# One fused graph network on one core: the opening and the convolution with degrees put in another order

## The chip, the cores and the metric

The kernel runs on one core of a Trainium2 chip. Its time is the device time in microseconds of one launch; lower is better. Several runs of the same program give a median. Besides the runs there is one profiled execution, whose trace lists every instruction of the engines: TensorE (PE, and PEld for its weight loads), VectorE (DVE), ScalarE (ACT), GpSimd (POOL) and SyncE (SP, which here only issues transfers). Each engine takes its own instructions strictly in order, as the kernel's lists stand, and waits for the others by semaphores.

## The reference, cut to what matters

512 nodes with 512 features, 16,896 edges sorted by destination. Four blocks follow each other, each with a residual:

```python
h = relu(layernorm(x)); x = x + attention_block(h, adjacency)      # L0: a graph transformer
h = relu(layernorm(x)); x = x + gin_block(h, edges)                # L1: sums over neighbours, two layers
h = relu(layernorm(x)); x = x + gcn(h, edges)                      # L2: convolution with degrees
h = relu(layernorm(x)); x = x + rgcn(h, edges, edge_types)         # L3: relations with 30 bases

def gcn(X, W, b, edge_index):        # loops are appended to the edges
    deg = segment_sum(1, dst);  dinv = rsqrt(deg)
    out = segment_sum((X @ W)[src] * dinv[src] * dinv[dst], dst) + b
    return where(out >= 0, out, 0.01 * out)
```

The relational block needs a weight matrix for each relation, which is a sum over 30 basis matrices of 512 x 512 (60 MB for its two layers).

## The kernel before, in words

**Edges become count matrices.** The kernel turns the edge list into dense 512 x 512 count matrices, one for each edge type, and every block then multiplies by them. For each chunk of 128 edges it makes two one-hot blocks, `hd` (destinations, 32 or 64 columns, on VectorE) and `hs` (sources, 512 columns, on ScalarE for four chunks in seven, on VectorE for three). A count matmul (`count`, line 556) multiplies them into a PSUM bank. There are 132 chunks and 204 count matmuls. The rows are made up to `BEHIND` = 7 chunks ahead of the counts.

**Stray edges.** Since the edges are sorted, each chunk is matched against only some groups of 32 destinations. `lim` holds the lowest and highest destination that a chunk may have, and `look_for_strays` (lines 406 to 420) sets `flag` if any edge lies outside. Line 460 reads the flag on all engines, and a branch leads to a slow path, which these inputs don't take. What follows in program order can't start on an engine before that engine has read the flag.

**The opening.** Around that check stand: the casts of the index (line 390) and their transposes into `key`; moments of the four tiles of x (lines 342 and 343); `first_norm` (a root, two small VectorE instructions and the normed tile `h`, lines 378 to 381); `flip`, which transposes a tile with four matmuls (line 331) and evicts it with ScalarE (line 335). GpSimd fills `lim`, adds the tile's offset to three parts of it (line 144), counts out `it` (line 150) and fills `apart` with ones (line 459). VectorE casts `it` into `iot` (line 415), the row that all one-hot blocks are compared with.

**Counts beside projections.** The loop over counts also carries the rest of the attention block's beginning. `plan` says after which count which piece comes: "p" half a tile of the projections q, k and v (lines 478 and 491, four passes of fp32 each), "G" a basis step, "s" and "S" scores. The first piece stands after count number `FIRST`, the others are spread evenly from there to the end of the counts. In the first eleven counts the planner of the framework may order instructions by its own costs; after that, and wherever an instruction is wrapped in `on(...)`, program order holds.

**Basis tiles.** SyncE streams the basis matrices in a fixed order through four buffers of 1 MB; the next load starts when a buffer is free. `basis_step` multiplies a tile into the PSUM bank `bas` (line 242). After the last step of a bank, ScalarE evicts it (line 247) and issues a DMA of 256 KB from its own queue (line 248). Other basis tiles are summed by VectorE (line 266).

**Convolution with degrees** (lines 1017 to 1060). It follows the second layer of L1, whose `settle` adds the last slices to x (line 855). The last basis step of that layer and the gate rows (line 803) come first. Then for every tile t of x: moments, a root (lines 1034 and 1045), `by = dinv / root` and `nm = -mean * by` (lines 1036 to 1038), the normed tile twice on ScalarE (line 1043: once rounded to fp32r as the high part, once in full), and the difference as the low part on VectorE (line 1046). `gather` (line 941) multiplies high and low parts of two tiles with the counts into the four `acc` banks. ScalarE and VectorE then copy the banks (lines 1053 and 1055) for the product with W.

## Time and profile before

| | |
|---|---|
| Median of three runs | 510.85 us (510.64 to 511.44) |
| Profiled execution, its own time | 512.15 us |
| Its span in the trace | 510.2 us |
| TensorE busy | 482.8 us (95%) |
| VectorE busy | 399.8 us (78%) |
| ScalarE busy | 196.1 us (38%) |
| GpSimd busy | 37.8 us (7%) |
| Moved by DMA | 94.06 MB, mean 184 GB/s |

The span runs from the first instruction of the trace to the last; the rest of the profiled execution's time lies around it. In the profile a name such as `hs<-iot,key` is output and inputs of an instruction; L547 is line 547 of the kernel before. The row of 40 slices gives the busy share of an engine in tenths, each slice 12.76 us long. A timeline has start, length, engine, line, operation and count, and in brackets how long the engine was idle before it and what ended that. A list of waits has the waiting instruction, the one waited for, the sum of the time, how often, and the longest.

### The profile page before, as it was taken

The page shows a single profiled execution, that of the slowest core. Times are in us where ns is not written, and L with a number is a line of the kernel's source. Part 1 is how long each engine was busy: PE and PEld are TensorE (multiplying, and loading weights), DVE is VectorE, ACT ScalarE, POOL GpSimd, SP SyncE. Part 2 cuts the span into 40 slices and gives each one's busy share as a digit, 9 for nine tenths or more (in the row PEclk, how much of TensorE's full clock was granted, in tenths as well). Part 3 has the DMA queues.
Part 4 walks back from the last instruction along what each step waited for, and adds up shares of the span by engine and source line. Part 5 has one row for each costly group of instructions (what it writes and reads, how often), then busy time and mean ns, then how long its engine had stood idle before and what let it go on. Part 6 is the DMA issues. An engine that isn't in the chain of part 4 may idle for free.

```text
span 510.2 us, 5732 instructions
## 1 busy us (share of the span) xinstructions
PE 482.8 (95%) x2014; PEld 247.4 (48%) x2014; DVE 399.8 (78%) x748; ACT 196.1 (38%) x318; POOL 37.8 (7%) x81
## 2 busy tenths in 40 slices
PE   2999999999999999999999999998699999999996
PEld 2333333255564547864445445543454584446642
DVE  6847487879999879999885964897459999998611
ACT  4876779724444213223422134124633610123000
POOL 7000000100000021300130000000010100000000
PEclk9999999999999999999999999999999999999999
DMA  7999768998978499686552696877933966520011
GB/s 244 273 249 258 176 175 195 218 261 192 226 162 193 109 214 297 226 216 228 189 176 83 153 233 213 293 198 188 255 103 124 308 177 222 180 82 3 0 42 41
DMA packets 42951, 94.06 MB, mean 184 GB/s; under 512 B 2113, under 2 KB 2567, under 8 KB 42919
## 3 DMA queue, kind: packets, MB, share of 16 engines
q1 hardware_dynamic: 34682, 68.17, 50.5%
q0 software_dynamic: 5712, 21.07, 14.2%
q10 hardware_dynamic: 2525, 4.39, 2.6%
q8 instruction: 20, 0.33, 0.3%
q14 instruction: 12, 0.10, 0.1%
HBM read 88.38 MB, written 5.24 MB: 183 GB/s over the span
## 4 chain that ended last, share of the span: by engine, by line
PE 65%; DVE 18%; ACT 9%; DMA 3%; issue 2%; ACTq 0%; DVEq 0%; SPq 0%
PE pr L318 19%; PE acc L1125 11%; PE pg L318 9%; PE acc L1091 5%; PE ps L478 4%; DMA basis<-in_basis 3%; PE bas L242 3%; DVE sc L642 3%; ACT sc L643 3%; ACT hs L547 3%; DVE sc L660 3%; PE ao L556 2%; PE acc L941 2%; DVE half L636 2%; DVE wrel L266 2%
## 5 line engine op out<-in xcount | busy, mean ns | idle before, releaser
L266 DVE SCALAR_TENSOR_TENSOR wrel<-basis,scal,wrel 128x1024 f32<-128x1024 f32 x60 | 74.1, 1282 | 2.5 <-DMA basis<-in_basis 2.5
L547 ACT ACTIVATE hs<-iot,key 128x512 f16<-128x512 f16 x75 | 48.8, 712 | 5.7 <-PE ao L556 4.9
L543 DVE TENSOR_SCALAR hd<-iot,key 128x32 f16<-128x32 f16 (+1 forms) x132 | 33.4, 295 | 15.6 <-PE ao L556 15.4
L242 PE MATMUL bas<-basis,wide 120*32 120x512 f32 (+1 forms) x320 | 43.5, 600 | 1.6 <-DMA basis<-in_basis 0.9
L266 DVE SCALAR_TENSOR_TENSOR w<-basis,scal,w 128x1024 f32<-128x1024 f32 x32 | 39.3, 1277 | 0.0
L556 PE MATMUL ao<-hs,hd 128*32 128x512 f16 x204 | 25.9, 396 | 2.8 <-ACT hs L547 2.6
L643 ACT ACTIVATE sc<-sc 128x2048 f32<-128x2048 f32 (+1 forms) x10 | 15.7, 1568 | 32.7 <-DVE sc L642 32.6
L478 PE MATMUL ps<-bigB,w 128*128 128x512 f32 x56 | 27.2, 614 | 0.9 <-ACT bigD L481 0.6
L318 PE MATMUL pr<-bigE,w 128*128 128x512 f32 x48 | 21.6, 596 | 0.0
L1175 DVE TENSOR_TENSOR u<-acc,x 128x512 f32<-128x512 f32 (+1 forms) x5 | 2.8, 584 | 23.5 <-PE acc L1125 23.5
L318 PE MATMUL pr<-bigD,w 128*128 128x256 f32 x88 | 20.2, 380 | 0.0
L549 DVE TENSOR_SCALAR hs<-iot,key 128x512 f16<-128x512 f16 x57 | 19.3, 347 | 0.0
L642 DVE TENSOR_TENSOR sc<-sc,half 128x2048 f32<-128x2048 f32 (+1 forms) x10 | 18.6, 1864 | 0.2
L660 DVE TENSOR_TENSOR sc<-sc,rec 128x2048 f32<-128x2048 f32 x8 | 18.3, 2286 | 0.0
L627 PE MATMUL psc<-bigC,bigD 64*128 64x256 f32 x128 | 18.1, 402 | 0.0
L318 PEld LDWEIGHTS pr<-bigD,w 128*128 128x128 f32 x88 | 16.6, 190 | 3.0 <-ACT bigE L885 0.8
L556 PEld LDWEIGHTS <-hd 128*32 128x32 f16 x204 | 6.1, 94 | 24.4 <-issue 15.7
L350 ACT ACTIVATE sd<-mv,eps 128x1 f32<-128x1 f32 x16 | 4.7, 296 | 34.4 <-DVE mv L343 33.4
L318 PE MATMUL pr<-w,bigE 128*128 128x512 f32 x40 | 17.8, 592 | 0.0
L658 DVE RECIPROCAL rec<-ps 128x256 f32<-128x256 f32 x8 | 14.0, 1752 | 3.7 <-PE ps L654 3.7
L478 PEld LDWEIGHTS ps<-bigB,w 128*128 128x128 f32 x56 | 9.6, 189 | 14.9 <-issue 11.1
L629 ACT COPY sc<-psc 128x1024 f32<-128x1024 f32 x16 | 15.6, 1007 | 2.6 <-issue 1.6
(317 smaller groups left out, 958.1 us busy)
## 6 DMA issues: line engine op xcount, KB each, us to landing
basis<-in_basis SPq DMA_DIRECT2D x32, 960.0 KB
basis<-in_basis SPq DMA_DIRECT2D x23, 1024.0 KB
basis<-in_basis SPq DMA_DIRECT2D x16, 448.0 KB
summed<-sums ACTq DMA_DIRECT2D x16, 256.0 KB
w<-in_W POOLq DMA_DIRECT2D x4, 1024.0 KB, 7.1
row<-in_rows POOLq DMA_DIRECT2D x12, 256.0 KB, 8.0
wrel<-summed POOLq DMA_DIRECT2D x4, 512.0 KB, 7.9
w<-in_conv_W1T POOLq DMA_DIRECT2D x2, 1024.0 KB, 5.9
```

The source lines that it names most:

```text
L242: tc.keep_in_program_order(nc.tensor.matmul(sums[0][32 * j:32 * j + 32, :], lhsT=lhsT, rhs=t[:k, j, :], start=(g == 0), stop=(g == STEPS + ...
L266: on(nc.vector.scalar_tensor_tensor(to[r][:, i:i + 2, :], t[:, i:i + 2, :], scal[:, at:at + 1], to[r][:, i:i + 2, :], op0=ALU.mult, op1=AL ...
L318: nc.tensor.matmul(p, lhsT=lhsT, rhs=rhs, start=(i == 0), stop=(i == len(pairs) - 1))
L478: on(nc.tensor.matmul(p, lhsT=w[:, k, ts(m)], rhs=made["hT"][:, k, :], start=(k == 0), stop=(k == T - 1)))
L543: keep(nc.vector.tensor_scalar(hd[:, :w], iot[:, GW * groups_of[c][0]:GW * groups_of[c][0] + w], key[:, 0, c:c + 1], key[:, 2, c:c + 1], o ...
L547: keep(nc.scalar.activation(hs, iot, AF.Sign, bias=key[:, 3, c:c + 1]))
L556: keep(nc.tensor.matmul(cnt[b][GW * (g % T):GW * (g % T) + GW, :], lhsT=hd[:, at:at + GW], rhs=hs, start=(c == in_bank[g][b][0]), stop=(c ...
L642: on(nc.vector.tensor_sub(s, s, half[:, 0:1, :].to_broadcast([P, H // pieces, NH])))
L643: on(nc.scalar.activation(s, s, AF.Exp, scale=HD ** -0.5))
L660: on(nc.vector.tensor_mul(self.sc, self.sc, rec[:, None, :].to_broadcast([P, H, NH])))
L1091: nc.tensor.matmul(self.out[t], lhsT=self.hT[:, k, ts(t)], rhs=self.root[:, k, :], start=(k == 0), stop=False)
L1125: nc.tensor.matmul(self.out[t], lhsT=self.uT[r][:, k, ts(t)], rhs=wrel[r][:, k, :], start=False, stop=(r == 1 and k == T - 1))
```

## The change

In the opening:

- GpSimd's arithmetic goes. The additions to `lim` move to VectorE ahead of everything else there; `apart` is filled by a ScalarE activation (the root of 0 times eps plus 1); the third cast of the index and `iot` go to ScalarE too.
- All four tiles of x are normed and transposed ahead of the check for strays, in written order. The roots are taken out of `first_norm` into `root`.
- The check compares with a fused operation for each end (`tensor_tensor_reduce`, largest excess in `some`), and two one-column matmuls add both. The upper limit becomes inclusive for it. The slow path makes its own list of strays.
- All counts are in program order, the first eleven too, and so is `select`, which prepares the weights of the basis steps. `FIRST` becomes 4.
- The first bias rows are asked for later in the program.

In the convolution with degrees:

- The last basis step stands behind the gate rows, and its eviction and DMA (`leave`) behind the whole norm.
- Moments and roots run ahead over all four tiles, high parts follow two tiles behind; then full parts and differences of tiles 0 and 1, a gather, both parts of tiles 2 and 3, a gather.

The diff, cut to its core (`on(...)` around instructions of `select`, and the slow path, are left out):

```diff
-        nc.gpsimd.tensor_scalar_add(over_tiles[:, :, t, :], over_tiles[:, :, t, :], float(P * t))
+        on(nc.vector.tensor_scalar_add(over_tiles[:, :, t, :], over_tiles[:, :, t, :], float(P * t)))
...
-    rows = Stream([row_load(i) for i in range(len(ROWS))], 4)
+    rows = Stream([row_load(i) for i in range(len(ROWS))], 0)
+    rows.ahead = 4
...
+                def leave(n=n, bank=sums[0]):
+                    o = spool.tile([P, 512], F32, tag="sums", name="sums")
+                    keep(nc.scalar.copy(o, bank))
+                    nc.scalar.dma_start(summed[l][n], o)
+
+                if held is None:
+                    leave()
+                else:
+                    held.append(leave)
...
+    def root(t):
+        on(nc.scalar.activation(by4[:, t, 0:1], mv4[:, t, 1:2], AF.Sqrt, bias=eps))
...
+    on(nc.scalar.activation(apart.rearrange("p t n -> p (t n)"), eps.to_broadcast([P, T * N]), AF.Sqrt,
+                            bias=ones, scale=0.0))
     for i in range(3):
-        on(nc.vector.tensor_copy(kn[:, i, :], idx[:, i, :]))
+        on((nc.scalar.copy if i == 2 else nc.vector.tensor_copy)(kn[:, i, :], idx[:, i, :]))
...
+    on(nc.scalar.copy(iot, it))
     moments(mv4[:, 0, :], x[:, 0, :], on)
+    root(0)
     on(nc.vector.tensor_copy(key[:, 0:2, :], pk[:, 0:2, :]))
     on(nc.vector.tensor_scalar(key[:, 2, :], pk[:, 2, :], 0.0, LESS, op0=ALU.is_equal, op1=ALU.max))
     moments(mv4[:, 1, :], x[:, 1, :], on)
-    for t in range(2):
-        first_norm(t)
+    first_norm(0)
+    root(1)
     moments(mv4[:, 2, :], x[:, 2, :], on)
+    root(2)
+    first_norm(1)
+    flip(h, 0, hT0, on)
+    moments(mv4[:, 3, :], x[:, 3, :], on)
+    root(3)
+    first_norm(2)
+    first_norm(3)
+    flip(h, 1, hT0, on)
+    on(nc.vector.tensor_scalar(key[:, 3, :], key[:, 1, :], -1.0, 0.5, op0=ALU.mult, op1=ALU.add))
...
+    some = rp.tile([P, 2], F32, name="some")
+    for i, ends in enumerate(((lim[:, 0, :], key[:, 0, :]), (key[:, 0, :], lim[:, 1, :]))):
+        on(nc.vector.tensor_tensor_reduce(stray, *ends, 1.0, 0.0, op0=ALU.subtract, op1=ALU.max,
+                                          accum_out=some[:, i:i + 1]))
+    for t in (2, 3):
+        flip(h, t, hT0, on)
+    p = ps()
+    for i in range(2):
+        on(nc.tensor.matmul(p[0:1, 0:1], lhsT=some[:, i:i + 1], rhs=ones, start=(i == 0), stop=(i == 1)))
+    on(nc.vector.tensor_copy(flag, p[0:1, 0:1]))
...
-    nc.gpsimd.memset(apart, 1.0)
...
     bases.start(AHEAD)
+    rows.start(4)
...
-    made["h"], made["hT"] = h, big("B")
-    for t in range(T):
-        flip(made["h"], t, made["hT"])
+    made["h"], made["hT"] = h, hT0
...
-    FIRST = 9
+    FIRST = 4
...
-        keep = on if n > 10 else loose
...
         if l:
-            basis_step(1)
+            held = []
             gates = gate_rows(1, [apart.bitcast(F32).rearrange("p t n -> p (t n)")[:, N * r:N * r + N] for r in range(2)])
             next(gates)
+            basis_step(1, on, held)
...
     for t in range(T):
+        moments(mv[:, t, :], x[:, t, :], on)
+        root(t)
+        if t:
+            scale(t - 1)
+        if t > 1:
+            normed_to(xn[0], t - 2)
+    scale(3)
+    for t in (0, 1):
+        normed_to(h, t)
         on(nc.vector.tensor_sub(xn[1][:, t, :], h[:, t, :], f32(xn[0][:, t, :])))
-        if t % 2:
-            gather((t - 1, t), apart=True)
+    gather((0, 1), apart=True)
+    for to in (xn[0], h):
+        for t in (2, 3):
+            normed_to(to, t)
+    for t in (2, 3):
+        on(nc.vector.tensor_sub(xn[1][:, t, :], h[:, t, :], f32(xn[0][:, t, :])))
+    gather((2, 3), apart=True)
+    for leave in held:
+        leave()
```

In the new convolution `root(t)` is the square root of a tile's variance, `scale(t)` the three small VectorE instructions for `by` and `nm`, and `normed_to(to, t)` one activation that writes the normed tile into the high part or in full into `h`.

## The prediction

> **What bounds the kernel now.** I read the page's busy rows and slices first, then the windows by stage, then the timeline at the two places that the change touches, then who waited there.

> ```profile
> span 510.2 us, 5732 instructions
> PE 482.8 (95%) x2014; PEld 247.4 (48%) x2014; DVE 399.8 (78%) x748; ACT 196.1 (38%) x318; POOL 37.8 (7%) x81
> PE   2999999999999999999999999998699999999996
> ```

> TensorE is busy 482.8 of 510.2 us, so 27.4 us are idle. The row of slices shows two dips: the first slice (0 to 12.8 us) and the slices near 360 us. These are the two places that the change rewrites. Everywhere else the order of instructions is kept, apart from where projections fall between counts, and TensorE stays the bound, so a shift made at either place should travel to the end.

> ```profile
> core 0: us, PE busy (x) PEld busy (x) DVE busy (x) ACT busy (x) POOL busy (x), PEclk, DMA share, GB/s
> 12.00:24.00 12.00, 11.06 (x38) 4.23 (x39) 10.33 (x58) 9.08 (x16) 1.01 (x5) 1.00 1.02 284
> 24.00:44.00 20.00, 19.46 (x90) 6.65 (x90) 11.93 (x46) 14.73 (x25) 0.77 (x1) 1.00 1.00 248
> ...
> 356.00:372.30 16.30, 11.34 (x58) 8.09 (x59) 8.37 (x26) 9.34 (x17) 0.00 (x0) 1.00 1.00 258
> ```

> From 24 us on TensorE idles 0.5 us in 20, while VectorE has 8 us to spare. In the convolution with degrees (356 to 372.3) TensorE idles 5 of 16.3 us. The waits of that stretch say on whom:

> ```profile
> PE acc L941 <- ACT bigC L1043: 4.6, 3, 1.9
> ```

> The timeline of the convolution (start, length, engine, line):

> ```profile
> 355.42 0.69 DVE L855 TENSOR_TENSOR x<-x,pg 128x512 f32<-128x512 f32 x1 [1.60 <-PE pg L331]
> 356.31 1.07 PE L242 MATMUL bas<-basis,wide 112*32 112x512 f32 x8 [0.93 <-DMA basis<-in_basis]
> 357.43 0.59 ACT L247 COPY sums<-bas 128x512 f32<-128x512 f32 x1 [2.76 <-PE bas L242]
> 358.42 0.48 ACT L1034 ACTIVATE sd<-mv,eps 128x1 f32<-128x1 f32 x2 [0.40 <-ACT sums L247]
> 359.39 0.81 ACT L1043 ACTIVATE bigC<-x,nm,by 128x512 fp32r<-128x512 f32 x1 [0.49 <-DVE nm L1038]
> 368.38 0.81 ACT L1043 ACTIVATE bigC<-x,nm,by 128x512 fp32r<-128x512 f32 x1 [1.27 <-DVE nm L1038]
> 370.32 1.98 PE L941 MATMUL acc<-R,F 128*128 128x512 f32 x8
> ```

> The last slice of x is whole at 356.11. The first square root waits for the eviction of the basis bank (line 247) to 358.42, and then each of the four tiles passes root, scale, high part, full part and difference nearly one after another, at about 3 us a tile. TensorE ends at 372.30.

> The opening, same columns:

> ```profile
> 10.51 0.14 DVE L418 CAST flag<-ps 1x1 int32<-1x1 f32 x1
> 12.07 1.09 PE L331 MATMUL ps<-ident,bigA 128*128 128x128 f32 x4 [1.86 <-DVEq L461]
> 13.09 0.62 PE L556 MATMUL ao<-hs,hd 128*32 128x512 f16 x3
> 14.45 0.59 PE L556 MATMUL ao<-hs,hd 128*32 128x512 f16 x1 [0.75 <-ACT hs L547]
> 17.35 3.68 PE L478 MATMUL psc<-bigB,w 128*128 128x512 f32 x4
> 21.29 1.98 PE L478 MATMUL psc<-bigB,w 128*128 128x512 f32 x4
> ```

> The flag is out at 10.65 and every engine reads it: TensorE resumes 1.42 later. Counts start at 13.09, with gaps and two transposed tiles among them.

> **The change, part 1: the convolution.** I walk the new order with the durations of the rows above, from x whole at 356.11. VectorE: moments of a tile take 0.9 (statistics 0.69, aggregation 0.18), a scale 0.6 (three small instructions, 358.75 to 359.35). Order: moments 0, 1, scale 0, moments 2, scale 1, moments 3, scales 2 and 3. Moments end at 357.05, 357.85, 359.3 and 360.65; scale 0 at 358.47, scale 1 at 359.85. ScalarE now has nothing of the basis bank ahead of it, but its order is root 0, 1, 2, then high part 0: root 2 waits for moments 2, so high part 0, ready at 358.5, goes at 359.6 (1.1 us given away) and ends at 360.4. Root 3 waits until 360.67, high part 1 ends at 361.8. From there six activations back to back, 0.72 apart as at 365.58 and 366.30: full parts 0 and 1 by 363.1, high parts 2 and 3 by 364.6, full parts 2 and 3 by 366.0. Differences (0.69): 363.15, 363.85, 366.0, 366.7.
> TensorE, four matmuls at 0.23 to 0.25 a piece (12 took 2.96): high 0 360.4 to 361.4; high 1 361.8 to 362.75; low 0 363.15 to 364.1; low 1 to 365.05; high 2 and 3 to 366.95; low 2 and 3 to 368.85. Against 372.30 that is **-3.4 us**. Bounds: the 28 matmuls after high 1 make 6.6 us, so no better than 368.4 (-3.9); with 0.3 us lost at each of three handovers, -2.5.
> The basis step itself moves behind the gate rows on TensorE, still ahead of the gathering matmuls. It waits for a load that landed at 356.2 and lasts 1.07; the first gathering matmul wants TensorE at 360.4, so the load may be 3.1 us later before it costs. Its eviction and its DMA (0.59 and 0.33 on ScalarE's queue) now stand behind full part 3, at 366.0 to 366.95, and ahead of two gate copies (1.05) to 368.0; the copy of the first sum wants ScalarE at 368.15. The cover is thus 0.15 us, and a slip costs its own length. Nothing reads that bank before 387.75, where the next basis bank begins.

> **Part 2: the opening, what is hidden.** GpSimd's three additions to lim (1.71 us in all) go to VectorE ahead of the casts, in time when it waits for the index until 3.20; three instructions of at most 0.3 us from 2.1 on. The row of the casts:

> ```profile
> L390 DVE CAST kn<-idx x3: 312/315/931, 3.2 to 4.3; 66x256 f32<-66x256 int32 x3
> ```

> The one cast that ran beside GpSimd's additions (2.75 to 4.46) took 0.93 instead of 0.31. If they were the cause, 0.6 us of VectorE comes back, plus 0.31 for the cast that moves; I count nothing of it on the path, since what follows waits for x and ScalarE (at most -0.2).
> ScalarE takes the fill of apart (1.91, by the 128x2048 exponential), a cast of 256 columns (0.38, from 0.59 at 512 and 1.01 at 1024) and iot (0.59). It sat idle 2.68 to 5.63. Starting behind ones at about 2.75, this ends at 5.65, and root 0 at 5.95; its reader comes at 6.84. Uncovered, these would cost up to 0.9.
> The check loses four operations (1.13) for two fused ones with a read each (0.36 at the price of L408's row, 0.76 at that of the 512-wide row of L1085: 0.72 to 1.5 together). They end near 12 us, under transposes: nothing. GpSimd's small iotas, the fifth row's DMA and SP's third basis load pass ahead of the flag; none has a reader before 17 us, and SP's queue is full until 22 us either way.

> **Part 3: the opening, what is on the path.** All four norms and transposes now stand ahead of the flag. From 7.26 (norm 0) ScalarE runs in order: norm 0 to 8.05, roots 1 and 2 to 8.65, norm 1 8.8 to 9.55, copy 0 to 10.15, root 3 to 10.45, norm 2 to 11.2, norm 3 to 11.95, copies 1 and 2 to 13.1. Transposes of a tile took 1.0 to 1.1: tile 2 11.2 to 12.3, tile 3 to 13.35. The flag's matmuls are queued behind tile 3 on TensorE, and all engines behind the flag: matmuls (0.2) and cast give 13.75, plus the 1.4 read 15.15, against 12.05 before: **3.1 us later**.
> What comes back: transposes of tiles 2 and 3 (2 x 1.1) and most of TensorE's gaps of 12 to 17.35 (0.9) are no longer behind the flag. With FIRST = 4 five counts, not eleven, precede the first projection. Rows come at about 0.4 us a chunk, so the fifth count ends near 17.45 and the first projection starts where it did (17.35). Compared at the third projection: before, it began at 23.81 with 21 counts done; after, first projection to 21.05, five counts 0.55, second 1.93, six counts 0.65: 24.2, with 16 done. Behind by 0.4 plus 5 x 0.11: **+1.0 us**.
> The clock speaks against the change here. The row: the first four projection matmuls took 3.68 us, the next four 1.98, and the halving falls at about 21.1, while the profile's granted clock reads 1.00 throughout. [...] I take +0.3, near the row. Opening: **+1.3**, between -0.2 (the cast's time comes back and more gaps close) and +2.6.

> **Sum.** Profiled execution: 512.15, span 510.20, 1.95 around it. Span 510.20 - 3.4 + 1.3 = 508.1. The median of the runs is 510.85, 1.3 below the profiled execution; applied there: 510.85 - 2.1 = **508.75**. Differences under 0.2% (1.0 us) are about what a measurement can't tell from no change.

> **Rivals.**
> *The opening costs about nothing* (chance 0.17). For: VectorE waits 15.4 us for TensorE to free one-hot rows later on, so a late supply catches up. Against: the flag is 3.1 later. 510.85 - 3.4 = 507.4.
> *The convolution gains little* (0.13), because ScalarE's strict order or the basis load holds TensorE. For: root 2 stands ahead of high part 0, and DMA is at 1.00 of its share in this window. Against: the load has 3.1 us of room. With 1.3 left of the gain, 510.8.
> *The late flag is lost whole* (0.15, the other side): dense work begins later, with transposes that had filled TensorE's gaps. [...]

> **How the numbers follow.** My case has 0.55, with its own range 507.7 to 509.8. The interval for 8 in 10 takes in the free opening and the little-gain case, and part of the late flag's: 506.9 to 511.4. Faster: 0.55 x 0.95 + 0.17 = 0.69; within 0.2%: 0.14; slower: 0.17 (the last rival, and 0.02 for what I overlook).

> **What would show it.** Right: the flag's cast near 13.75 and counts from 15.5; first projection near 17.45; third near 24.2; in the convolution about 12.7 us from x whole to the last gathering matmul, instead of 16.2, with TensorE idle under 2.5 us. Wrong: projections of 3.6 us beyond 21.5, gaps among counts from 24 on, a basis matmul that waits past x whole + 3 us, or the gain of the convolution met by a new wait for basis tiles near 310 or past 390.

## The result, and the profile after

| | before | after |
|---|---|---|
| Median of six runs | 511.14 us (510.3 to 511.73) | 514.75 us (513.85 to 516.05) |
| Profiled execution, its own time | 512.15 us | 514.07 us |
| Its span | 510.2 us | 511.6 us |

The ratio is 1.0067, with a 95% interval of 1.0051 to 1.0083: the changed kernel is slower, by 3.4 us of 511. The forecast was 508.75, within 506.9 to 511.4.

The page's busy row and slices of the kernel after:

```profile
span 511.6 us, 5740 instructions
PE 483.0 (94%) x2016; PEld 247.3 (48%) x2016; DVE 399.4 (78%) x749; ACT 198.4 (39%) x321; POOL 34.4 (7%) x77
PE   2899998899999999999999999899799999999997
```

TensorE's work is the same (483.0 against 482.8 us), so what is lost is idle time. New are an eight in the second slice, two in the seventh and eighth (77 to 102 us), where the change moves nothing but the places of the pieces of the plan, and one in the 26th (320 to 333 us), where the change moves nothing. By stages:

```profile
core 0: us, PE busy (x) PEld busy (x) DVE busy (x) ACT busy (x) POOL busy (x), PEclk, DMA share, GB/s
12.00:24.00 12.00, 9.34 (x37) 4.29 (x38) 8.26 (x42) 8.02 (x13) 0.00 (x0) 1.00 1.02 308
24.00:44.00 20.00, 18.76 (x84) 6.27 (x85) 12.91 (x57) 15.40 (x27) 0.76 (x1) 1.00 0.93 236
...
361.03:373.65 12.62, 10.13 (x52) 7.15 (x51) 8.10 (x25) 9.02 (x17) 0.00 (x0) 1.00 1.03 252
```

TensorE idles 2.7 of the 12 us up to 24, where it idled 0.9 before, and 1.2 instead of 0.5 us in the twenty after that; it goes on losing until about 105. The convolution with degrees takes 12.62 us from x whole to the last gathering matmul; before it was 16.19.

The timeline of the opening after (columns as before):

```profile
10.55 0.69 DVE L349 BATCH_NORM_STATS2 st<-x 128x6 f32<-128x512 f32 x1 [1.02 <-DMA x<-in_x]
14.84 0.15 DVE L434 CAST flag<-psc 1x1 int32<-1x1 f32 x1 [1.92 <-PE psc L433]
15.77 3.78 ACT L562 ACTIVATE hs<-iot,key 128x512 f16<-128x512 f16 x6 [0.52 <-ACT bigB L342]
16.80 1.48 PE L571 MATMUL ao<-hs,hd 128*32 128x512 f16 x5 [2.00 <-DVE hs L564]
18.21 2.73 PE L493 MATMUL psc<-bigB,w 128*128 128x512 f32 x4
21.41 1.98 PE L493 MATMUL psc<-bigB,w 128*128 128x512 f32 x4
```

VectorE gets the last tile of x only at 10.55, the cast of the flag starts at 14.84, and behind it TensorE stands two more microseconds until the first one-hot rows are there: no row was made before the flag. The convolution after:

```profile
360.34 0.69 DVE L867 TENSOR_TENSOR x<-x,pg 128x512 f32<-128x512 f32 x1 [1.60 <-PE pg L338]
362.01 0.29 ACT L1045 ACTIVATE sds<-mvs,eps 128x1 f32<-128x1 f32 x1 [2.42 <-DVE mvs L350]
362.02 1.06 PE L247 MATMUL bas<-basis,wide 112*32 112x512 f32 x8
364.31 0.80 ACT L1053 ACTIVATE bigC<-x,nms,bys 128x512 fp32r<-128x512 f32 x1
365.25 2.46 PE L953 MATMUL acc<-R,bigC 128*128 128x512 f32 x8 [2.17 <-ACT bigC L1053]
367.90 2.12 PE L953 MATMUL acc<-R,F 128*128 128x512 f32 x8 [0.18 <-DVE F L1065]
369.85 1.98 PE L953 MATMUL acc<-R,bigC 128*128 128x512 f32 x8
371.67 1.98 PE L953 MATMUL acc<-R,F 128*128 128x512 f32 x8
```

The first root starts 0.98 after x is whole instead of 2.31 and waits for its moments, not for the basis bank. Once the gather runs, TensorE has gaps of 0.18 us at most.

Before the experiments, one milestone that they share: the 12 matmuls that sum the weights of the first attention block (line 654 before, 669 after), the last piece of the plan, behind count 193. I call their start "the sums". The profiled executions reach it at 102.18 (before) and 105.56 (after): 3.38 us later. From there to x whole after takes 1.54 us longer, the convolution 3.57 less, and the rest to the end of the execution 0.57 longer, which makes the 1.92 between the two executions. Of this last term 0.54 lies outside the span of the trace: time less span is 2.4 to 2.7 us in all six runs of the changed kernel and 1.9 to 2.0 in those of the kernel before. With the old convolution in the changed kernel it is 1.8 to 2.0; no experiment told its cause.

### The profile page after: what moved, and what is told of

The parts are those of the page before. It is cut to its first block, busy times and chain, and to the rows that moved or that the text cites. A ratio compares the mean times of both kernels' runs of the same rounds, so it can differ in the third digit from the quotient of the medians.

```text
span 511.6 us, 5740 instructions
## 1 busy us (share of the span) xinstructions
PE 483.0 (94%) x2016; PEld 247.3 (48%) x2016; DVE 399.4 (78%) x749; ACT 198.4 (39%) x321; POOL 34.4 (7%) x77
## 3 DMA queue, kind: packets, MB, share of 16 engines
q0 software_dynamic: 5712, 21.07, 13.8%
## 4 chain that ended last, share of the span: by engine, by line
PE 64%; DVE 20%; ACT 7%; issue 2%; DMA 2%; DVEq 0%; ACTq 0%
PE pr L329 19%; PE acc L1151 11%; PE pg L329 10%; PE acc L1117 5%; PE ps L493 4%; DVE sc L657 3%; ACT sc L658 3%; PE bas L247 3%; DVE sc L675 3%; PE acc L953 3%; ACT hs L562 2%; DMA basis<-in_basis 2%; DVE half L651 2%; PE ao L571 1%; PE psc L793 1%
## 5 line engine op out<-in xcount | busy, mean ns | idle before, releaser
L558 DVE TENSOR_SCALAR hd<-iot,key 128x32 f16<-128x32 f16 (+1 forms) x132 | 33.5, 293 | 15.4 <-PE ao L571 14.9
L247 PE MATMUL bas<-basis,wide 120*32 120x512 f32 (+1 forms) x320 | 43.3, 601 | 0.7 <-ACT sums L253 0.7
L506 PE MATMUL ps<-w,bigB 128*128 128x512 f32 x32 | 15.9, 618 | 1.0 <-DVE bigE L509 1.0
```

The costliest lines, as they stand in the source:

```text
L247: tc.keep_in_program_order(nc.tensor.matmul(sums[0][32 * j:32 * j + 32, :], lhsT=lhsT, rhs=t[:k, j, :], start=(g == 0), stop=(g == STEPS + ...
L558: keep(nc.vector.tensor_scalar(hd[:, :w], iot[:, GW * groups_of[c][0]:GW * groups_of[c][0] + w], key[:, 0, c:c + 1], key[:, 2, c:c + 1], o ...
```

## The experiments

The ratios are to runs of the kernel before beside them on the same chip (its median was 510.93 to 511.71 there). Microseconds are made from ratios, at 511 for the whole, since not all kernels ran beside each other.

| Kernel | Median, us | Ratio (95%) | us |
|---|---|---|---|
| before + new convolution | 508.82 | 0.9953 (0.9938 to 0.9969) | -2.4 |
| after, old convolution | 516.94 | 1.0109 (1.0090 to 1.0128) | +5.6 |
| after, FIRST = 9 | 511.77 | 1.0018 (1.0009 to 1.0028) | +0.9 |
| before, FIRST = 4 | 513.31 | 1.0039 (1.0025 to 1.0052) | +2.0 |
| after, FIRST = 9, check early | 514.93 | 1.0065 (1.0049 to 1.0081) | +3.3 |
| new convolution + written order | 512.55 | 1.0023 (1.0015 to 1.0031) | +1.2 |
| new convolution + arithmetic moved | 514.67 | 1.0062 (1.0043 to 1.0080) | +3.2 |
| new convolution + early pieces, first attempt | 509.41 | 0.9958 (0.9944 to 0.9973) | -2.1 |
| after, FIRST = 9, rows between norms | 511.50 | 1.0003 (0.9989 to 1.0016) | +0.2 |
| new convolution + FIRST = 4, pair at 49 | 511.17 | 0.9993 (0.9979 to 1.0008) | -0.4 |
| new convolution + early pieces | 509.30 | 0.9951 (0.9933 to 0.9970) | -2.5 |
| new convolution + late pieces | 512.15 | 1.0006 (0.9993 to 1.0019) | +0.3 |
| after, early pieces only | 512.68 | 1.0020 (1.0008 to 1.0032) | +1.0 |
| new convolution, roots later | 508.16 | 0.9932 (0.9916 to 0.9949) | -3.5 |
| the same again | 507.92 | 0.9926 (0.9908 to 0.9945) | -3.8 |
| the same + idle matmuls | 508.66 | 0.9945 (0.9926 to 0.9965) | -2.8 |

### The three parts, one at a time

The kernel before with the part of the diff behind `settle` and in `basis_step` alone (`held`, `leave`, roots and moments ahead, gathers in pairs):

```diff
-            basis_step(1)
+            held = []
...
+            basis_step(1, on, held)
...
+    gather((0, 1), apart=True)
...
+    gather((2, 3), apart=True)
+    for leave in held:
+        leave()
```

> The kernel before with the new order of the convolution alone. Theory: the gain in the convolution stands by itself. From x whole to the last gathering matmul 12.6 us, as in the changed kernel, instead of 16.2: 3.6 us less than before, about 507.3, and the waits for basis tiles near 310 us as before (2.5 us on VectorE). Rival: the order pays only where the basis load behind it lands early; then the basis matmul ahead of the gather waits and the gain is under 1.5 us.

The changed kernel without that part:

> The changed kernel with the old convolution. Theory: the opening and the counts cost 3.4 us by the end of the counts (sums of the first block at 105.6 instead of 102.2) and nothing later, so 3.4 us more than before. Rival: the longer wait for the basis tile near 315 us (4.1 us on VectorE instead of 2.5) belongs to the opening too: then 5 us more.

The changed kernel with the old first place of the projections:

```diff
-    FIRST = 4
+    FIRST = 9
```

> The changed kernel with FIRST = 9 again. Theory of the plan: the 2 us that are lost between 24 us and the end of the counts come from the earlier projections, so the counts end 1.0 to 1.4 us later than before instead of 3.4, and the time is 2 us below that of the changed kernel. Rival, supply: rows begin 3.6 us later and the counts never have their lead again, whatever FIRST is: the time of the changed kernel within 0.5 us, and the counts end 3.4 us later than before.

And the kernel before with the new one:

```diff
-    FIRST = 9
+    FIRST = 4
```

> The kernel before with FIRST = 4 alone. Theory of the plan: the counts end about 2 us later and the time is 2 us more. Rival, supply: within 0.5 us of before.

Measured: the convolution brings 2.4 us and not 3.4, between its theory and its rival; the opening as a whole costs 5.6 (after with the old convolution, nearer to the rival's 5 than to the theory's 3.4) to 5.8 (1.0067 less 0.9953) and not 1.3. Of this, FIRST = 4 is 2.5 in the changed kernel (1.0067 less 1.0018) and 2.0 in the kernel before; the rest of the opening is 3.3 (1.0018 less 0.9953). Convolution -2.4, rest of the opening +3.3, FIRST +2.5: as differences of the same ratios they must add up to the 3.4; what checks them is that the parts measured alone, 5.6 and 2.0, lie near 5.8 and 2.5. With FIRST = 9 the time is the theory's, but the milestone is the rival's: the sums stand at 105.74 in its profiled execution, and at 105.56 with FIRST = 4. The first of these executions is 1.9 us above the median of its kernel, the second 0.7 below, so this pair can't show the 2.5 us of the runs. Three questions follow, one for each part.

### Why the rest of the opening costs 3.3 us

First theory: the flag waits for the last tile of x and for all transposes. The check was put ahead of the last two tiles:

```diff
+    for i, ends in enumerate(((lim[:, 0, :], key[:, 0, :]), (key[:, 0, :], lim[:, 1, :]))):
+        on(nc.vector.tensor_tensor_reduce(stray, *ends, ...))
     moments(mv4[:, 2, :], x[:, 2, :], on)
...
+    on(nc.vector.tensor_copy(flag, p[0:1, 0:1]))
+    flip(h, 0, hT0, on)
+    flip(h, 1, hT0, on)
+    first_norm(2)
...
     rows.start(4)
+    flip(h, 2, hT0, on)
+    moments(mv4[:, 3, :], x[:, 3, :], on)
+    root(3)
+    first_norm(3)
+    flip(h, 3, hT0, on)
```

> The changed kernel with FIRST = 9, whose check for strays again comes ahead of the last two tiles: the compares right behind the index, the flag's matmuls and cast behind the norm of tile 1; tiles 2 and 3 are transposed behind the read of the flag (tile 3 normed there too). All else of the opening stays: arithmetic on ScalarE and VectorE, all counts in program order. With FIRST = 9 the changed kernel took 511.8 us, and the kernel before with the new convolution 508.8: 3.0 us lie in the opening. Theory (the flag waits for the last tile of x and for all transposes, and stands at 14.8 to 16.3 us instead of 10.5): the flag's cast comes back to 10 to 11.5, and the time to 509.5 us (509.0 to 510.2). Rival (strict order of the first eleven counts, or the fills and casts on ScalarE): the flag comes early, and the time stays at 511.3 to 512.2.

Rivals of it were the written order by itself, and the arithmetic by itself:

```diff
-        keep = on if n > 10 else loose
...
-            rows_of(needed[made_rows], keep)
+            rows_of(needed[made_rows], on)
...
-        count(g, c, cnt, keep)
+        count(g, c, cnt, on)
```

> The kernel before with the new convolution (508.8 us), and of the new opening only the written order: the first eleven counts, their one-hot rows and the selection of weights keep program order, so that all four transposed tiles stand ahead of the first count. Theory of the late flag: this costs at most 0.5 us, as the transposes have to be made anyway: 508.8 to 509.4. [...]

```diff
-        nc.gpsimd.tensor_scalar_add(over_tiles[:, :, t, :], over_tiles[:, :, t, :], float(P * t))
+        on(nc.vector.tensor_scalar_add(over_tiles[:, :, t, :], over_tiles[:, :, t, :], float(P * t)))
...
-    nc.gpsimd.memset(apart, 1.0)
+    on(nc.scalar.activation(apart.rearrange("p t n -> p (t n)"), ..., AF.Sqrt, bias=ones, scale=0.0))
...
-        on(nc.vector.tensor_copy(iot, it))
+    on(nc.scalar.copy(iot, it))
```

> The kernel before with the new convolution (508.8 us), and of the new opening only the places of the arithmetic: the additions to the limits on VectorE, and the fill of ones, the third cast of the index and the row of column numbers on ScalarE. The order of norms, check and flag is that of before. Theory of the late flag: ScalarE is idle until 5.6 us and takes these in cover: 508.5 to 509.1. Rival (ScalarE's 2.9 us of added work stands ahead of the roots and of the first one-hot rows): flag 1 us later, 509.8 to 511.

None of the three came out as the theory of the late flag had it. The flag did come early in the first (11.2 us), and the kernel became 2.4 us slower still (1.0065 against 1.0018), not faster. The written order alone costs 3.6 us (1.0023 less 0.9953), as much as the rest of the opening loses, with the flag at 10.7 where it always was. Its timeline of TensorE:

```profile
12.89 1.09 PE L337 MATMUL ps<-ident,bigA 128*128 128x128 f32 x4 [2.62 <-DVEq L467]
15.36 1.11 PE L337 MATMUL psc<-ident,bigA 128*128 128x128 f32 x4 [1.39 <-ACT bigA L387]
16.40 0.62 PE L562 MATMUL ao<-hs,hd 128*32 128x512 f16 x3
17.77 2.23 PE L562 MATMUL ao<-hs,hd 128*32 128x512 f16 x7 [0.75 <-ACT hs L553]
19.93 2.08 PE L484 MATMUL psc<-bigB,w 128*128 128x512 f32 x2
```

Here all transposes come first and the first count starts at 16.40, not at 13.1. The planner of the kernel before had woven the first counts and rows in between: ScalarE made its first row at 13.67, ahead of the norm of the last tile; in written order it makes none until all norms and evictions are through. What the kernels with the same places of pieces have in common (us of one profiled execution each):

| | flag | ScalarE's first row | first projection | sums | difference of the last two |
|---|---|---|---|---|---|
| new convolution | 10.5 | 13.67 | 17.34 | 101.38 | 84.04 |
| + written order | 10.7 | 16.99 | 19.93 | 105.31 | 85.38 |
| after, FIRST = 9 | 16.1 | 17.05 | 21.05 | 105.74 | 84.69 |
| + arithmetic moved | 12.7 | 15.15 | 21.72 | 106.58 | 84.86 |
| after, check early | 11.2 | 19.55 | 22.49 | 107.04 | 84.55 |

The flag does not order these kernels; the first projection does, and everything behind it takes 84.0 to 85.4 us whatever went before. It stands behind ten or eleven counts and the last transposed tile, and so waits for the last engine that serves either.

Most of the spread in the last column is the clock. The records of the granted clock begin, in each trace, where TensorE comes to full speed: in the kernel before at 20.79, and the matmuls of its projections start 0.85 us apart ahead of that and 0.43 behind it. In the five kernels this is at 19.23, 24.34, 23.96, 24.97 and 25.11. An estimate of 83.1 us, fitted to the first kernel, plus half the time from the first projection to there gives 84.0, 85.3, 84.6, 84.7 and 84.4 for the column. So of the 3.9 us that the written order loses by the sums, 1.3 is the clock in these two executions, and 2.6 the later first projection.

Two of the five are not clean tests. In the early check I wrote the root of the last tile behind three evictions on ScalarE (16.28), so its norm and rows came later than before. In the kernel with the arithmetic moved, the planner, free to do so, used the early `iot` to pull eight `hd` rows and half of `select` ahead of VectorE's reading of the flag; with two transposes behind the last norm ahead of TensorE's reading of it, TensorE went on at 16.83 instead of 12.07. That kernel is 5.6 us slower than without (1.0062 less 0.9953), beyond its rival's expectation too, so what the moved arithmetic costs by itself is not shown; the changed kernel with FIRST = 9, at 1.0018 against 1.0023 for the written order alone, leaves little for it.

If the law holds, rows made between the norms must bring the time back:

```diff
+    flip(h, 0, hT0, on)
+    more_rows(2)
+    flip(h, 1, hT0, on)
+    more_rows(1)
+    moments(mv4[:, 2, :], x[:, 2, :], on)
+    root(2)
+    first_norm(2)
+    more_rows(1)
...
     for n, (t, g, c) in enumerate(order):
```

> The changed kernel with FIRST = 9 (511.8 us), the written order kept for everything, but written otherwise: the check and the read of the flag come behind the norm of tile 1, before tiles 2 and 3 are looked at, and the one-hot rows of the first eight chunks stand between the norms and transposes instead of behind them all. Theory (what decides is when the first ten counts are done, and in the written order of the change no row is made before all norms and evictions: first projection at 21.05 us instead of 17.34, which passes on whole): first projection at 16 to 18, sums at its start + 84.8, time 508 to 509.5 us. Rival (ScalarE's fills and casts, or the asking for bias rows, cost by themselves): 511 or more although the first projection is early.

The timeline of that kernel:

```profile
8.08 0.11 DVE L423 CAST flag<-ps 1x1 int32<-1x1 f32 x1
12.12 0.72 ACT L552 ACTIVATE hs<-iot,key 128x512 f16<-128x512 f16 x1
17.52 1.46 PE L561 MATMUL ao<-hs,hd 128*32 128x512 f16 x10
18.91 2.67 PE L483 MATMUL psc<-bigB,w 128*128 128x512 f32 x4
```

The ten counts now run through without a wait (1.46 instead of 3.04 us), but the first projection stands at 18.91, not at 16 to 18: tiles 2 and 3 still pass root, scale and norm one after another, with rows between. The sums follow at 102.86, 83.95 later, as the law has it. That is 2.9 us earlier than with FIRST = 9 alone, 0.7 of it by the clock (full speed 1.4 us after the first projection, against 2.9). The time, though, is the rival's (511 or more): 0.8 us better than without (1.0003 against 1.0018, the intervals overlap). The profiled executions are 3.0 apart (513.65 and 510.62), but neither is a run of the middle: 513.65 is 1.9 above its median, 510.62 is 0.9 below. Both kernels spread over more than 3 us, and the table above compares single executions, not medians. So the traces show that the first projection orders the sums, and the test of the written order shows that it costs 3.6 us; that rows between the norms bring this back, the runs don't show.

### Why FIRST = 4 costs 2.5 us

Theory from the plan: with 9, two half projections stand at the end of the first tile (count 49) and cover the eviction of its banks; with 4 only one does. Three kernels take the plan apart, on the kernel before with the new convolution. The first attempt at early pieces:

```diff
+        first = 4 if i < 5 else FIRST
-        at = max(at, FIRST + (len(order) - 2 - FIRST) * passes // whole)
+        at = max(at, first + (len(order) - 2 - first) * passes // whole)
```

> The kernel before with the new convolution (508.8 us, FIRST = 9), where only the first five half projections take the places that FIRST = 4 gives them (behind counts 4, 9, 15, 21, 27); from the first basis step on all pieces stand where FIRST = 9 puts them. FIRST = 4 alone cost 2.4 us on the kernel before, 3.0 in the changed one. Theory (the pieces further back are what costs: with FIRST = 9 two half projections stand at the end of the first 50 counts and cover the eviction of their banks, with FIRST = 4 one does): 508.8 to 509.5. Rival (the first projection at half rate comes ahead of more one-hot rows, which then lack supply): 510.8 to 512.

This edit left the loop's starting point at 9, so that the first piece stayed behind count 9, beside the second; only pieces two to five moved. They cost nothing. With FIRST = 4 and the pair put back:

```diff
-        at = next((e for e in ends if abs(at - e) < 7), at)
+        at = next((e for e in ends if abs(at - e) < 7), 49 if at == 41 else at)
```

> The kernel before with the new convolution (508.8 us) and FIRST = 4 (alone 2.4 us dearer, so 511.2 expected without more), where only the half projection that FIRST = 4 puts behind count 41 goes to the end of the first tile (count 49) again, as with FIRST = 9, so that two half projections stand there. Theory of the pair (the missing cover at that end is the whole cost): 508.8 to 509.6. Rival (the cost is spread: each of the later halves meets an eviction that ScalarE or VectorE hasn't done, 0.5 us in each of the stretches 54 to 64, 74 to 84 and 94 to 104 us): 510.4 to 511.4.

The pair is not the cause: 2.0 us of the loss stay (0.9993 less 0.9953). Then the early half and the late half of the plan, each alone:

```diff
-    plan, passes, at, halves = {}, 0, FIRST, 0
+    plan, passes, at, halves = {}, 0, 4, 0
...
+        first = 4 if i < 5 else FIRST
```

> The kernel before with the new convolution (2.1 us faster than before), where the first five half projections stand behind counts 4, 9, 15, 21 and 27, the first too (early4 had left it behind 9), and all others where FIRST = 9 puts them. Theory (the later places cost): 1.5 to 2.5 us faster than before. Rival (the first piece, a projection at half rate ahead of six counts, costs): 0.5 us faster to 0.5 slower.

```diff
+        first = FIRST if i < 5 else 4
```

> The kernel before with the new convolution (2.1 us faster than before), where the first five half projections stand where FIRST = 9 puts them, and all later pieces where FIRST = 4 puts them, from the first basis step (33 instead of 37) on. Theory (the later places cost 2.4 us, the early ones nothing): 0.5 us slower to 0.5 us faster than before. Rival (the early ones cost): 1.5 to 2.5 us faster than before.

The early pieces are free (0.9951), the late ones cost 2.7 us (1.0006 less 0.9953). But the first piece did not move in the second attempt either: in its trace the first two halves stand together behind eleven counts (17.32, eight matmuls), and so they do in the kernel before with FIRST = 4, since the planner still orders the first eleven counts of the old opening. What is free is the second to fifth piece; the first is tested in the changed opening, at the end of this section.

Windows of the kernel with the late pieces:

```profile
54.00:64.00 10.00, 9.48 (x57) 3.50 (x49) 5.20 (x18) 8.02 (x15) 0.76 (x1) 1.00 0.71 171
74.00:84.00 10.00, 8.46 (x51) 3.15 (x50) 8.66 (x30) 9.63 (x13) 0.00 (x0) 1.00 0.88 206
94.00:104.00 10.00, 8.53 (x45) 2.79 (x38) 7.73 (x25) 8.08 (x13) 1.29 (x2) 1.00 0.99 224
```

and of the kernel with the new convolution alone:

```profile
54.00:64.00 10.00, 9.98 (x57) 3.65 (x49) 5.84 (x21) 7.37 (x13) 0.76 (x1) 1.00 0.71 168
74.00:84.00 10.00, 9.02 (x52) 3.35 (x50) 6.47 (x23) 9.62 (x15) 0.00 (x0) 1.00 0.93 217
94.00:104.00 10.00, 9.30 (x44) 4.24 (x42) 5.81 (x21) 6.17 (x10) 1.29 (x2) 1.00 1.00 264
```

TensorE idles 1.83 us more in these three stretches, and the sums come 1.92 later (103.30 against 101.38). The waits of TensorE from 24 to 106 us say for what; with the late pieces (sum, times, longest):

```profile
PE ps L497 <- DVE bigE L500: 1.0, 2, 0.6
PE ps L484 <- ACT bigD L487: 1.0, 3, 0.5
PE ps L484 <- ACT bigC L487: 0.6, 2, 0.3
```

and without:

```profile
PE ps L484 <- ACT bigD L487: 0.6, 2, 0.4
PE ps L484 <- ACT bigC L487: 0.3, 1, 0.3
PE ps L497 <- DVE bigE L500: 0.2, 1, 0.2
```

The sum of the three is 2.6 against 1.1 us. A half projection shares the bank `ps` with the one ahead of it, and waits when VectorE or ScalarE has not evicted that yet. Places up to four counts earlier are enough: each such wait is 0.2 to 0.6 us. The kernel after shows the same rows with 1.0, 1.0 and 0.5, with FIRST = 9 they are 0.2, 0.6 and 0.2. These waits are thus 1.5 of the 1.9 us by the sums. The rest of the 2.7 of the runs is not told apart; this trace loses 2.0 us more between the sums and x whole, in the wait of the last section of experiments.

Do the early pieces at least help where rows are late, as the prediction had it?

```diff
-    FIRST = 4
+    FIRST = 9
...
-    plan, passes, at, halves = {}, 0, FIRST, 0
+    plan, passes, at, halves = {}, 0, 4, 0
...
+        first = 4 if i < 5 else FIRST
```

> The changed kernel with only the first five half projections at the places of FIRST = 4, all later pieces at those of FIRST = 9. With FIRST = 4 for all it was 3.6 us slower than before, with FIRST = 9 for all 0.8 slower. Theory of the loan (the early pieces use TensorE while rows are still being made, as the prediction had it, and the later places of FIRST = 4 give that back): 0.5 us faster than before to 0.5 slower. Rival (early pieces bring nothing even in a late opening): 0.8 to 1.5 slower. Second rival (the early pieces themselves cost in this opening): 2.5 or more slower.

Not in the runs: 1.0020 against 1.0018 without them, the first rival. The lead at the third projection is real in the trace (25.39 with 16 counts done, against 27.38 with 21), and by the sums 0.8 us of it are left in these two executions (104.93 against 105.74). 0.6 us of what is lost is found: TensorE waits 0.6 for an `hd` of VectorE between 24 and 34 us, a wait that the kernel with FIRST = 9 doesn't have. Where the rest goes, and why the medians show no lead at all, stays open.

### Why the convolution brings 2.4 us and not 3.4

In the traces of the kernels with the new convolution the stretch from x whole to the last gathering matmul is 12.60 to 12.62 us in three (after, written order, first attempt at early pieces; mean granted clock 0.999 to 1.0) and 13.32 to 13.82 in nine (mean clock 0.996 or 0.997). The records of the granted clock show why. They lie on a grid: in each of the eleven traces with a half clock near x whole, two of them with the old convolution, it lasts 3.41 us and begins a whole number of times 3.413 us (100 to 104) behind the first record. Two windows of that grid in the kernel before with the new convolution, whose stretch is 13.72:

```profile
357.15:360.56 3.41, 1.16 (x4) 0.69 (x5) 2.98 (x14) 2.12 (x5) 0.00 (x0) 1.00 1.05 270
360.56:363.97 3.41, 3.39 (x8) 2.73 (x9) 1.39 (x2) 3.41 (x6) 0.00 (x0) 0.50 1.05 231
```

and in the kernel after, whose stretch is 12.62:

```profile
361.08:364.49 3.41, 2.00 (x18) 0.97 (x16) 3.17 (x13) 0.97 (x4) 0.00 (x0) 1.00 1.01 342
364.49:367.91 3.42, 2.33 (x9) 1.35 (x9) 2.46 (x11) 3.12 (x6) 0.00 (x0) 1.00 1.07 228
```

In the first TensorE works 1.16 of 3.41 us, and then gets half clock (0.50) for the next 3.41, inside the gather: its third group, of eight matmuls, takes 2.73 us, in the kernel after 2.12. In the second the grid cuts the same idle time in two, no window has less than 2.00 us of work, and the clock stays. So it is in all eighteen traces: ahead of a half clock near x whole the window has 1.16 to 1.76 us of work (eleven traces), and where none comes, the emptiest window there has 1.8 to 3.0 (seven). One window elsewhere, at 322 us of the kernel with the late pieces, has 1.72 and keeps the full clock, so the limit is not sharp. Where the grid lies differs from trace to trace (first records at 16.0 to 25.1 us).

The old convolution has a trace without half clock (before, 16.19) and two with it (15.63 and 15.87), and shows no loss by it. The mean over the twelve new traces is 13.34, over the three old ones 15.90: 2.6 apart, near the 2.4 of the runs.

The runs bear this out in part. Of the kernel before with the new convolution, the two runs at a mean clock of 0.999 took 508.68 and 508.96 us, and the four at 0.996 and 0.997 took 508.31 to 509.15: no difference. Over the eleven kernels with the new convolution that have runs of both kinds, those at 0.997 or less took 0.8 us longer on the average. So half clock is a part of what the convolution falls short by; that it is the whole is not shown.

The walk had also named 1.1 us that ScalarE gives away, because root 2 stands ahead of high part 0:

```diff
         if t:
             scale(t - 1)
-        if t > 1:
-            normed_to(xn[0], t - 2)
+        if t in (1, 2):
+            normed_to(xn[0], t - 1)
```

> The kernel before with the new convolution (508.8 us), where in its norm the high part of a tile follows its scale at once, ahead of the next root (high part 0 before root 2, high part 1 before root 3). The prediction's walk has ScalarE give away 1.1 us there: high part 1 would end at 360.6 instead of 361.8, and the 28 matmuls behind it (6.6 us) set the end. Theory of the walk: 0.7 us less, 508.1 (507.8 to 508.5). Rival (the low parts or the clock set the end): no change, 508.7 to 509.2.

The stretch is 11.90 us, the 0.7 less that the walk gives; by the runs the kernel gains 1.1 us (0.9932 less 0.9953, the intervals overlap). To see whether TensorE's idle time ahead of the gather brings the half clock, the same kernel ran again beside one that fills it:

> The same kernel as conv_roots, again, beside the next one: 3.0 to 3.6 us faster than before. Where a run's mean granted clock is 0.996 or 0.997, its span is expected about 1.1 us longer than where it is 0.999 or 1.0.

```diff
+    p = bank(turn[0][(turn[1] + 1) % len(turn[0])])
+    for i in range(32):
+        on(nc.tensor.matmul(p[:, :P], lhsT=far_off, rhs=far_off, start=True, stop=True))
     for t in range(T):
         moments(mv[:, t, :], x[:, t, :], on)
```

> conv_roots with 32 matmuls of 128x128 bf16 that compute nothing (their bank is never read), put behind the last basis step, where TensorE otherwise idles until the first gathering matmul. Theory (too little work in the 4 us ahead of the gather brings half clock for 3.4 us in most runs, at 1.1 us each): the half clock in the gather is gone, the runs' mean clock is 0.999 or more, and the time is 0.5 to 1 us below conv_roots in the same hour. Rival (the half clock comes by chance, whatever TensorE does there, or the added matmuls hold the gather up): no change, or 0.3 to 1 us slower.

TensorE in the repeated kernel:

```profile
356.66 1.07 PE L242 MATMUL bas<-basis,wide 112*32 112x512 f32 x8
358.89 1.15 PE L947 MATMUL acc<-R,bigC 128*128 128x512 f32 x4 [1.17 <-ACT bigC L1047]
360.20 1.16 PE L947 MATMUL acc<-R,bigC 128*128 128x512 f32 x4 [0.16 <-ACT bigC L1047]
361.84 2.14 PE L947 MATMUL acc<-R,F 128*128 128x512 f32 x8 [0.48 <-DVE F L1059]
```

The filling brought nothing (11.93 against 11.95 us in the stretch, and 0.9945 against 0.9926, intervals overlapping; the medians are 0.7 us apart to its disadvantage), since nothing was left to take away: with the roots later, TensorE idles 1.17 us instead of 2.16 ahead of the gather, and all twelve runs of this kernel have a mean clock of 0.998 or more, where four of six had 0.996 or 0.997. The grid says the same: wherever it is laid over the two traces of this kernel, no window near x whole has less than 2.09 us of work, while over the trace of the new convolution alone 72% of its places have a window under 1.78 us. The shorter idle time thus keeps the clock up; that matmuls without use would have done it too was not tested on a kernel that had the half clock. The cost of half clock inside the repeated kernel could not be seen either, for want of a run that had it.

The kernel before with the new convolution and the roots later is the best one of all: 0.9932 and 0.9926 of the kernel before.

### A wait that comes and goes

From the sums to x whole, fourteen of the eighteen traces take 253.7 to 254.2 us, and four (after among them) 255.3 to 255.6. It is one wait, of VectorE for a basis tile, near 320 us; in the kernel after:

```profile
DVE wrel L277 <- DMA basis<-in_basis: 4.1, 1, 4.1
```

and in the kernel before:

```profile
DVE wrel L266 <- DMA basis<-in_basis: 2.5, 1, 2.5
```

In the four the wait is 3.8 to 4.2 us, in the others 2.0 to 2.7. Two of the four are the changed opening with FIRST = 4, one is the kernel with the late pieces, one the early check with FIRST = 9; the kernel before with FIRST = 4 doesn't have it. No experiment told its cause apart. It accounts for 1.5 us of the profiled execution after, and is no part of the differences of the medians that I can separate.

## Why the prediction was wrong

The forecast was a change of -2.1 us, and +3.4 was measured. Of the 5.5 between them, 1.0 lies in the convolution and 4.5 in the opening, where two steps of part 3 failed: "What comes back", which entered the written order as a gain, and "Compared at the third projection", which put the later pieces of the plan at nothing.

- **The convolution, -3.4.** The mechanism was right, step for step: the first high part was walked to begin 3.5 us after x whole and began 3.28 after, the last gathering matmul 12.7 and came at 12.62, the basis matmul waited for nothing. The term that was mis-sized is "TensorE, four matmuls at 0.23 to 0.25 a piece": in nine of the twelve traces half clock falls into the gather for 3.41 us, and the stretch is 13.3 to 13.8. The runs give -2.4, of which the half clock explains a part. The eviction of the basis bank behind the last full part, with its cover of 0.15, held nothing up.
- **The opening, what is hidden.** Fill and casts on ScalarE ended at 5.5, as walked (5.65). No clean test shows whether they cost nothing: the kernel made for it lost 5.6 us, with another order of the planner's. The two casts that stayed on VectorE took 0.29 and 0.69 us, so GpSimd's additions were not the whole cause of the slow one.
- **The opening, "3.1 us later".** The flag came 1.2 us later than walked, at 14.99 instead of 13.75. The walk has root 3, and so the moments of tile 3, done by 10.45; VectorE got that tile at 10.55. In the kernel with FIRST = 9 VectorE waited 3.09 us for one tile. In the kernel before it waited for none, but it read the last one only at 10.58, so its trace could not tell when that landed.
- **"What comes back".** This is the first step that failed. Transposes and gaps were credited with 2.2 and 0.9 us, so that the first projection would start where it did. The runs showed the reverse: in the kernel before the planner had put counts and rows between those transposes, and the written order, which I took for a form without price, costs 3.3 to 3.6 us. With FIRST = 9 the first projection starts at 21.05 instead of 17.35. The gaps named as gain were where rows were being made.
- **"Compared at the third projection ... +1.0 us".** This is the second. The comparison itself was good: third projection at 23.86 with 16 counts done, walked 24.2 (before, it began at 23.74, not at 23.81), and 1.05 us more idle time of TensorE by 24 us. But the five counts not yet done were entered at 0.11 us each, as if the rest of the plan ran as before. It does not: early pieces are worth nothing in the runs, and the later ones, which I had only shifted along, cost 2.7 us in the test of them alone, where waits for `ps` are 1.5 us of the 1.9 by the sums. FIRST = 4 as a whole costs 2.0 to 2.5. The walk stops at the third of forty pieces.
- **The clock, +0.3.** No run shows this term, nor the room for the clock in the upper end of the opening's range (+2.6); both were my estimates. Full speed came at 19.75 in the profiled execution, where the row had 21.1, and first between 16.0 and 25.1 in all eighteen. From the first projection on, half rate lasted 1.54 us there and 3.44 in that of the kernel before: by half of the difference, about 0.95 us, the clock was in the change's favour in this pair, by luck.
- **The rivals.** The rival on the other side, the late flag lost whole, had the right sign and nearly the right place: a delay ahead of the first projection passes on whole (between it and the sums lie 84.0 to 85.4 us in the five kernels of the table). Its carrier is not the flag, though. By the runs 3.3 is what the rest of the opening costs; half rate from the first projection on lasted 4.41 us in the execution with the written order and 1.54 in that of the changed kernel. The rival of a hidden opening was refuted by the same table. That the places of the later pieces could cost was in no case of mine, so no case reached 514.

## What to carry to other kernels

A scheduler's freedom near the start can be worth more than the instructions that are saved there: before fixing an order by hand, list what each engine does first in the planner's order, and keep the first work of the engine that everything downstream waits for (here ScalarE's one-hot rows) between the preparations, not behind them. A parameter that seems to move the first piece of an evenly spread plan moves every piece; look for the waits on shared banks along the whole of it. And compare at the end of the stage, not at the third milestone of it.

## What the runs showed of the hardware

At the start of the kernel the column of the granted clock reads 1.00 while a projection's matmuls take up to 3.78 us instead of 1.98, so it can't be read there: the records begin with the first change to full speed, at 16.0 to 25.1 us. The window ahead of that change had 2.95 to 3.41 us of work.

The tiles of x, four loads issued within 1.8 us, landed at different times in each execution. VectorE had to wait for the third until 10.46 with FIRST = 9, and had it at 7.97 in the changed kernel; in all it waited 3.9 and 2.4 us there, and not at all in the kernel before, where it wants the first and the last later. That this makes the spread of the times is not shown: the changed kernel with FIRST = 9 ran from 510.65 to 513.8 us, but the one with rows between the norms, whose flag is out at 8.19, ran from 510.16 to 513.57.
